# Sharing a weighted sum of gathered rows between VectorE and TensorE: more slots for TensorE in eight of 26 row tiles, another cut of the large tiles, and a new order at the end

## The chip, the cores and the metric

The kernel runs on one core of a Trainium2 chip. The metric is the device time of one execution in microseconds (us), the median of several runs. A core has engines that run side by side, each with its own in-order queue of instructions: TensorE (PE in the profile; its weight loads are a row of their own, PEld), VectorE (DVE), ScalarE (ACT), GpSimd (POOL) and SyncE (SP). Transfers run on 16 DMA engines. An engine waits for another through semaphores.

## The reference

A graph attention layer over 3327 nodes with 1024 features. The adjacency matrix is sparse: a node has between 1 and about 37 neighbours, itself included.

```python
def _L0_gnn_ref(x, adj, Wf, bf, Wg, bg, W, bW):
    f = x @ Wf + bf
    g = x @ Wg + bg
    e = jax.nn.relu(f @ g.T)
    scores = jnp.where(adj > 0, e, NEG)
    attention = jax.nn.softmax(scores, axis=1)
    x_W = x @ W + bW
    return attention @ x_W

h = jnp.maximum(_layernorm(x, axis=-1), 0.0)
x = x + _L0_gnn_ref(h, adj, ...)
```

## The kernel before

The kernel never forms the 3327 x 3327 scores. Its first part (up to about 260 us) reads x and adj, writes the normalised rows h to DRAM (`hd`), makes a list of neighbours for every row, and sorts the rows by their number of neighbours. The sorted rows are cut into 26 tiles of 128. Tile s needs `CAPS[s]` slots: slot k of a tile is the k-th neighbour of each of its 128 rows, and is fetched as one gather of 128 rows x 1024 f32 from `hd` into a buffer `G`. There are 26 such buffers.

For each tile the second part does this: `prepare` gathers the tile's own rows, transposes them on TensorE and multiplies them by A (made of Wf and Wg) to get q (24 matmuls); `dot` takes, for every slot, the dot product of the gathered row with q on VectorE; `softmax` turns the scores into weights; `combine` sums the gathered rows by their weights into y; `project` multiplies y by W (16 matmuls), and the residual x is added. A tile with more than 16 slots is done in two units, with a running softmax between them: y of the first unit is rescaled when the second unit's scores are known.

```python
CAPS = [37, 25, 23, 22, 21, 21, 20, 20, 19, 19, 18, 18, 17, 17, 17, 16, 16, 15, 15, 15, 14, 14, 13, 13, 12, 11]
ORDER = [24, *range(24), 25]
ONE_CHUNK = 16
AHEAD = 3
...
    gpool = ctx.enter_context(tc.tile_pool(name="G", bufs=26))
...
    def dot(s, k):
        e = st[s]
        g = G[s, k] = gpool.tile([P, D], FP, name="G")
        st["gathered"] = gather(g, hd[:, :], e["edges"][k])
        junk = jpool.tile([P, D], BF, name="junk")
        nc.vector.tensor_tensor_reduce(
            junk, g, e["q"][:, :D], 1.0, e["q"][:, D : D + 1], op0=ALU.mult, op1=ALU.add,
            accum_out=e["sc"][:, k : k + 1],
        )
...
    def on_tensor(s, k0, k1):
        m = min(max(0, CAPS[s] - 12), k1 - k0 - 2) if s != ORDER[0] else (k1 - k0) // 2
        ks = range(max(k0, 1), k1)
        return [k for i, k in enumerate(ks) if (i + 1) * m // len(ks) > i * m // len(ks)]

    def sum_transposed(e, g, first, last):
        ...
        for c in range(KD):          # KD = 8
            nc.tensor.matmul(
                e["yT"][:, c, :], g[:, c * P : (c + 1) * P], ident, is_transpose=True,
                start=(first and c % 4 == 0), stop=(last and c % 4 == 3), skip_group_check=True,
            )

    def combine(s, k0, k1, last):
        ...
        pe = on_tensor(s, k0, k1) if last else []
        for k in range(k0, k1):
            p = e["sc"][:, k : k + 1]
            g = G[s, k]
            if k in pe:
                nc.scalar.activation(g, g, AF.Copy, scale=p)
                sum_transposed(e, g, e["first"], False)
                e["first"] = False
            elif k == 0:
                nc.scalar.activation(y, y, AF.Copy, scale=p)
            else:
                nc.vector.scalar_tensor_tensor(y, g, p, y, op0=ALU.mult, op1=ALU.add)

    def project(s):
        e = st[s]
        yT = yTpool.tile([P, KD, P], FP, name="yT")
        sum_transposed(e, e["y"], e["first"], True)
        ...                          # copy yT_ps to yT, 16 matmuls by W_sb into ps_o, add x, scatter
```

So a slot's row is added in one of two ways. On VectorE, one `scalar_tensor_tensor` does y = g * p + y. On TensorE, ScalarE first scales the row by p, and eight 128 x 128 transposes add it, transposed, into the PSUM tile `yT`, where y itself is added at the end. `on_tensor` picks m slots of the last (or only) unit of a tile for the second way: CAPS - 12, but at most the unit's slots less two.

The units are made, and worked through, like this:

```python
    units = []
    for s in ORDER:
        cap = CAPS[s]
        half = (cap + 1) // 2
        units += [(s, 0, half), (s, half, cap)] if cap > ONE_CHUNK else [(s, 0, cap)]
    ...
    for i, (s, k0, k1) in enumerate(units):
        last = k1 == CAPS[s]
        at = ORDER.index(s)
        dots(s, range(k0, k1))
        softmax(s, k0, k1, last)
        if i + 1 < len(units):
            s2, a, b = units[i + 1]
            dots(s2, range(a, min(b, a + AHEAD)))
        if last and at:
            finish(ORDER[at - 1])
        combine(s, k0, k1, last)
        if last:
            project(s)
            if at + 2 < NT:
                prepare(ORDER[at + 2])
```

The queue of each engine is not in this order throughout: it is arranged when the program is built. The trace shows VectorE taking a sum of one unit and a dot of the next in turn.

Of the kernel before, what the change touches and what calls it, by code (L numbers as in the profile page):

```python
# [11 lines left out]
ALU = mybir.AluOpType  # L12
# [14 lines left out]
CAPS = [37, 25, 23, 22, 21, 21, 20, 20, 19, 19, 18, 18, 17, 17, 17, 16, 16, 15, 15, 15, 14, 14, 13, 13, 12, 11]  # L27

ORDER = [24, *range(24), 25]
ONE_CHUNK = 16  # L30
AHEAD = 3
LAG = 4

# [260 lines left out]
def edge_path(ctx: ExitStack, tc: tile.TileContext, x, adj, Wf, bf, Wg, bg, W, bW, out, flag):  # L294
# [11 lines left out]
    nc = tc.nc  # L306
    N, D = x.shape
# [43 lines left out]
    with ExitStack() as part1:  # L351
# [34 lines left out]
        half = c1.tile([P, 1], FP, name="half")  # L386
# [298 lines left out]
    def gather(to, table, idx, **kw):  # L685
        return nc.gpsimd.indirect_dma_start(  # L686
            out=to,
            out_offset=None,
            in_=table,
            in_offset=bass.IndirectOffsetOnAxis(ap=idx, axis=0),  # L690
            **kw,
        )
# [8 lines left out]
    st = {}  # L701
# [57 lines left out]

    G = {}  # L760

    def dot(s, k):
        e = st[s]
        g = G[s, k] = gpool.tile([P, D], FP, name="G")
        st["gathered"] = gather(g, hd[:, :], e["edges"][k])
        junk = jpool.tile([P, D], BF, name="junk")
        nc.vector.tensor_tensor_reduce(  # L767
            junk, g, e["q"][:, :D], 1.0, e["q"][:, D : D + 1], op0=ALU.mult, op1=ALU.add,
            accum_out=e["sc"][:, k : k + 1],
        )  # L770

    def dots_of_first(s, cap):

# [40 lines left out]

    def on_tensor(s, k0, k1):

        m = min(max(0, CAPS[s] - 12), k1 - k0 - 2) if s != ORDER[0] else (k1 - k0) // 2
        ks = range(max(k0, 1), k1)
        return [k for i, k in enumerate(ks) if (i + 1) * m // len(ks) > i * m // len(ks)]

    def sum_transposed(e, g, first, last):

        if first:
            e["yT"] = p_y.tile([P, KD, P], FP, name="yT_ps")
        for c in range(KD):
# [7 lines that stand above are left out]
        if not k0:  # L833
            e["y"] = G[s, 0]
        y = e["y"]
        e["first"] = True
# [8 lines that stand above are left out]
            elif k == 0:  # L845
                nc.scalar.activation(y, y, AF.Copy, scale=p)  # L846
            else:
                nc.vector.scalar_tensor_tensor(y, g, p, y, op0=ALU.mult, op1=ALU.add)  # L848

    def project(s):  # L850
        e = st[s]
# [51 lines left out]
    units = []  # L903
    for s in ORDER:
        cap = CAPS[s]
        half = (cap + 1) // 2
        units += [(s, 0, half), (s, half, cap)] if cap > ONE_CHUNK else [(s, 0, cap)]
    done = set()

    def dots(s, ks):  # L910
        for k in ks:
            if (s, k) not in done:
                done.add((s, k))
                dot(s, k)

    prepare(ORDER[0])
    prepare(ORDER[1])
# [2 lines left out]
# [15 lines that stand above are left out]
            if at + 2 == NT - 1:  # L935
                bad = failed()
# [4 lines left out]
def kernel(tc: tile.TileContext, x, adj, Wf, bf, Wg, bg, W, bW, out):  # L941

    nc = tc.nc
    with tc.tile_pool(name="flag", bufs=1) as fpool:
        flag = fpool.tile([1, 1], I32, name="flag")
        bad = edge_path(tc, x, adj, Wf, bf, Wg, bg, W, bW, out, flag)
        with tc.If(bad > 0):
            dense_path(tc, x, adj, Wf, bf, Wg, bg, W, bW, out)  # L950
# [27 lines left out]
```

## Time and profile before

| | |
|---|---|
| median of 3 runs | 1331.45 us (1329.03 to 1333.0) |
| profiled span | 1331.5 us |
| VectorE busy | 1184.0 us, 89% |
| TensorE busy, matmuls | 1105.4 us, 83% |
| ScalarE busy | 580.1 us, 44% |
| gathers of G by the lists (GpSimd) | 454, 1074 ns each |
| dots (L767) | 456, 1286 ns each |
| sums on VectorE (L848) | 296, 1289 ns each |
| row scalings for TensorE's slots (L842) | 146, 1136 ns each |
| transposes that add rows to yT (L826) | 1376 |

The profile is of one execution. A row of the groups gives the line of the kernel, the engine and operation, what is written and read, the count, then the busy time in us and the mean ns of one, then the idle time of that engine just ahead of them and what ended most of it. The row of 40 digits for an engine gives the busy tenths of 40 equal slices of the span, here 33.3 us each. TensorE's matmuls are shown in two records each for f32, and overlap: their pitch, from start to start, is shorter than one record.

### The profile page before, as it was taken

The page shows a single profiled execution, that of the slowest core. Times are in us where ns is not written, and L with a number is a line of the kernel's source. Part 1 is how long each engine was busy: PE and PEld are TensorE (multiplying, and loading weights), DVE is VectorE, ACT ScalarE, POOL GpSimd, SP SyncE. Part 2 cuts the span into 40 slices and gives each one's busy share as a digit, 9 for nine tenths or more (in the row PEclk, how much of TensorE's full clock was granted, in tenths as well). Part 3 has the DMA queues.
Part 4 walks back from the last instruction along what each step waited for, and adds up shares of the span by engine and source line. Part 5 has one row for each costly group of instructions (what it writes and reads, how often), then busy time and mean ns, then how long its engine had stood idle before and what let it go on. Part 6 is the DMA issues. An engine that isn't in the chain of part 4 may idle for free. (4 is left out here: it accounts for less than half of the span.)

```text
span 1331.5 us, 14117 instructions
## 1 busy us (share of the span) xinstructions
PE 1105.4 (83%) x4312; PEld 690.2 (52%) x4312; DVE 1184.0 (89%) x2377; ACT 580.1 (44%) x923; POOL 847.2 (64%) x677
## 2 busy tenths in 40 slices
PE   2588897289249899898999999999999997889965
PEld 2355564056136655566555656656556554545532
DVE  4779888749988999999999999999999998889990
ACT  6778787224125533555334444444433332224210
POOL 6699888356657766666666766666665655666511
PEclk9589898589669999999999999999999998899978
DMA  9999996398659988998899888988788776868811
GB/s 356 338 374 342 393 374 218 134 376 309 207 177 333 337 284 297 330 316 308 297 313 321 319 291 309 311 296 297 263 290 284 259 253 222 269 198 274 303 32 50
DMA packets 101660, 374.45 MB, mean 281 GB/s; under 512 B 14731, under 2 KB 18474, under 8 KB 98247
## 3 DMA queue, kind: packets, MB, share of 16 engines
q0 software_dynamic: 79584, 286.77, 63.4%
q1 hardware_dynamic: 11004, 71.01, 14.0%
q10 hardware_dynamic: 10986, 15.67, 3.3%
q8 instruction: 36, 0.59, 0.2%
q14 instruction: 50, 0.41, 0.1%
HBM read 344.11 MB, written 29.30 MB: 280 GB/s over the span
## 5 line engine op out<-in xcount | busy, mean ns | idle before, releaser
L686 POOL DMA_INDIRECT G<-hd,pi x454 | 487.4, 1074 | 199.2 <-issue 102.6
L767 DVE CUSTOM_DVE_ANT_0 junk<-G,q 128x1024 bf16<-128x1024 f32 x456 | 586.5, 1286 | 8.8 <-DMA G<-hd,pi 4.3
L731 PE MATMUL ps_q<-A_sb,hT 128*128 128x342 f32 x1248 | 382.1, 460 | 11.8 <-ACT hT L699 11.7
L848 DVE SCALAR_TENSOR_TENSOR G<-G,sc 128x1024 f32<-128x1024 f32 x296 | 381.4, 1289 | 10.6 <-ACT G L846 6.8
L861 PE MATMUL ps_o<-W_sb,yT 128*128 128x512 f32 x832 | 364.4, 596 | 7.9 <-ACT yT L855 7.9
L731 PEld LDWEIGHTS ps_q<-A_sb,hT 128*128 128x128 f32 x1248 | 236.2, 193 | 136.5 <-ACT hT L699 17.8
L861 PEld LDWEIGHTS ps_o<-W_sb,yT 128*128 128x128 f32 x832 | 158.0, 191 | 202.0 <-issue 187.5
L424 POOL TENSOR_TENSOR r<-r,iotaj 128x1664 f32<-128x1664 f32 (+3 forms) x52 | 191.6, 3724 | 31.9 <-ACT r L417 31.8
L826 PE MATMUL yT_ps<-ident,G 128*128 128x128 f32 x1376 | 172.5, 281 | 28.6 <-DVE G L848 15.3
L826 PEld LDWEIGHTS yT_ps<-ident,G 128*128 128x128 f32 x1376 | 155.8, 144 | 55.3 <-ACT G L842 26.4
L842 ACT ACTIVATE G<-G,sc 128x1024 f32<-128x1024 f32 x146 | 154.9, 1136 | 0.0
L475 DVE MAX8 cand<-r 128x8 f32<-128x208 f32 (+2 forms) x416 | 121.7, 360 | 29.0 <-POOL r L424 29.0
L551 PE MATMUL ps_A<-WgT,WfT 128*128 128x342 f32 x432 | 140.5, 485 | 0.2 <-ACT WfT L532 0.2
L870 ACT COPY res<-ps_o 128x512 f32<-128x512 f32 x50 | 29.2, 585 | 255.0 <-PE ps_o L861 252.8
L551 PEld LDWEIGHTS ps_A<-WgT,WfT 128*128 128x128 f32 x432 | 86.3, 205 | 60.5 <-issue 21.1
L735 ACT COPY q<-ps_q 128x342 f32<-128x342 f32 x78 | 34.3, 440 | 172.7 <-PE ps_q L731 158.7
L698 PE MATMUL ps_t<-ident,G 128*128 128x128 f32 x208 | 31.9, 303 | 80.1 <-DMA G<-hd,perm 67.5
L881 POOL DMA_INDIRECT out_dram<-res,perm x25 | 35.6, 1424 | 84.0 <-DMA res<-in_x_dram,perm 83.7
L417 ACT ACTIVATE r<-r 128x3327 f32<-128x3327 int32 (+4 forms) x28 | 77.8, 2781 | 1.5 <-ACT xt L461 0.5
L686 POOL DMA_INDIRECT res<-in_x_dram,perm x25 | 43.1, 1724 | 54.8 <-ACT res L870 49.9
L698 PEld LDWEIGHTS ps_t<-ident,G 128*128 128x128 f32 x208 | 27.3, 157 | 88.8 <-issue 74.5
L699 ACT COPY hT<-ps_t 128x512 f32<-128x512 f32 x52 | 29.2, 588 | 100.4 <-PE ps_t L698 100.4
(132 smaller groups left out, 669.4 us busy)
## 6 DMA issues: line engine op xcount, KB each, us to landing
r<-in_adj_dram SPq DMA_DIRECT2D x25, 1663.5 KB, 10.9
xt<-in_x_dram SPq DMA_DIRECT2D x25, 512.0 KB, 9.2
hd<-xt ACTq DMA_DIRECT2D x25, 512.0 KB, 7.7
G<-hd,pi POOLq DMA_INDIRECT x454, 6.2
wr<-in_L_gnn_Wg_dram SPq DMA_DIRECT2D x8, 512.0 KB, 5.8
wr<-in_L_gnn_Wf_dram SPq DMA_DIRECT2D x8, 512.0 KB, 8.1
W_sb<-in_L_gnn_W_dram SPq DMA_DIRECT2D x1, 4096.0 KB, 17.9
cd<-cand ACTq DMA_DIRECT2D x25, 64.0 KB, 7.6
```

The source lines that it names most:

```text
L417: nc.scalar.activation(r[:n, b:e], a[:n, b:e], AF.Sign, accum_out=to)
L424: nc.gpsimd.tensor_mul(r[:n, b:e], r[:n, b:e], iotaj[:n, : e - b])
L475: nc.vector.max(cand[:n, s * 8 : s * 8 + 8], r[:n, s * SW : min(N, (s + 1) * SW)])
L551: nc.tensor.matmul(ps[:, :QB], WfTs[c][:, k, :], WgT[:, k, o : o + QB], start=(k == 0), stop=(k == KD - 1))
L686: return nc.gpsimd.indirect_dma_start(out=to, out_offset=None, in_=table, in_offset=bass.IndirectOffsetOnAxis(ap=idx, axis=0), **kw,)
L698: nc.tensor.transpose(ps[:, k, :], of[:, (g + k) * P : (g + k + 1) * P], ident)
L731: nc.tensor.matmul(ps[:, :QB], hT[:, k, :], A_sb[:, k, o : o + QB], start=False, stop=(k == KD - 1), skip_group_check=True,)
L767: nc.vector.tensor_tensor_reduce(junk, g, e["q"][:, :D], 1.0, e["q"][:, D : D + 1], op0=ALU.mult, op1=ALU.add, accum_out=e["sc"][:, k : k ...
L826: nc.tensor.matmul(e["yT"][:, c, :], g[:, c * P : (c + 1) * P], ident, is_transpose=True, start=(first and c % 4 == 0), stop=(last and c % ...
L842: nc.scalar.activation(g, g, AF.Copy, scale=p)
L848: nc.vector.scalar_tensor_tensor(y, g, p, y, op0=ALU.mult, op1=ALU.add)
L861: nc.tensor.matmul(ps, yT[:, k, :], W_sb[:, k, o * CB : (o + 1) * CB], start=False, stop=(k == KD - 1), skip_group_check=True,)
```

## The change

It moves sums from VectorE to ScalarE and TensorE, and changes where a large tile is cut, so that its last unit has enough slots for TensorE's share. `FIRST` and `LARGEST` set the cut: the first unit has 10 slots, or more where the second would have over 22 (22 slots, y, and three slots of the next unit fill the 26 buffers). In the last two tiles of the order (23 and 25) the share is CAPS - 7 in place of CAPS - 12. For the last tile, the dots that are issued once the tile before has its sums are queued behind the last of those sums on VectorE.

```diff
+FIRST = 10
+LARGEST = 22
...
-    def dot(s, k):
+    def dot(s, k, behind=None):
...
-        nc.vector.tensor_tensor_reduce(
-            junk, g, e["q"][:, :D], 1.0, e["q"][:, D : D + 1], op0=ALU.mult, op1=ALU.add,
-            accum_out=e["sc"][:, k : k + 1],
-        )
+        with tc.issue_after(behind.ins) if behind else ExitStack():
+            nc.vector.tensor_tensor_reduce(
+                junk, g, e["q"][:, :D], 1.0, e["q"][:, D : D + 1], op0=ALU.mult, op1=ALU.add,
+                accum_out=e["sc"][:, k : k + 1],
+            )
...
-        m = min(max(0, CAPS[s] - 12), k1 - k0 - 2) if s != ORDER[0] else (k1 - k0) // 2
+        m = min(max(0, CAPS[s] - (7 if s in ORDER[-2:] else 12)), k1 - k0 - 2) if s != ORDER[0] else (k1 - k0) // 2
...
-                nc.vector.scalar_tensor_tensor(y, g, p, y, op0=ALU.mult, op1=ALU.add)
+                e["summed"] = nc.vector.scalar_tensor_tensor(y, g, p, y, op0=ALU.mult, op1=ALU.add)
...
-        half = (cap + 1) // 2
-        units += [(s, 0, half), (s, half, cap)] if cap > ONE_CHUNK else [(s, 0, cap)]
+        first = max(FIRST, cap - LARGEST)
+        units += [(s, 0, first), (s, first, cap)] if cap > ONE_CHUNK else [(s, 0, cap)]
...
-                dot(s, k)
+                dot(s, k, st[ORDER[-2]].get("summed") if s == ORDER[-1] else None)
```

## The prediction

> **What bounds the kernel now.** I read the page's busy tenths first, to find the stretches, and then the busy times by stretch, the groups, the waits, and the last 75 us instruction by instruction. The tenths:
>
> ```profile
> PE   2588897289249899898999999999999997889965
> DVE  4779888749988999999999999999999998889990
> PEclk9589898589669999999999999999999998899978
> ```
>
> Up to slice 8 (some 265 us) the change touches nothing. From slice 13 to 33 both VectorE and TensorE show 8 and 9; in 34 to 36 both dip; at the end VectorE falls to 0 while TensorE works on. Busy times of these stretches (columns: stretch, length, then PE, PEld, DVE, ACT, POOL, the granted clock, DMA share, GB/s):
>
> ```profile
> 385.00:440.00 55.00, 49.33 (x234) 33.85 (x234) 47.75 (x74) 27.83 (x39) 33.66 (x29) 0.93 0.78 260
> 440.00:660.00 220.00, 206.94 (x879) 134.03 (x878) 218.81 (x344) 99.14 (x157) 147.03 (x137) 0.98 0.90 313
> 660.00:960.00 300.00, 287.33 (x1207) 179.75 (x1206) 298.11 (x465) 139.68 (x225) 199.93 (x181) 0.99 0.89 305
> 960.00:1080.00 120.00, 115.58 (x425) 68.83 (x425) 113.27 (x157) 39.74 (x68) 75.07 (x69) 1.00 0.82 275
> 1080.00:1200.00 120.00, 100.42 (x363) 62.34 (x362) 99.30 (x145) 35.56 (x65) 67.70 (x56) 0.91 0.71 227
> 1258.00:1332.00 74.00, 47.59 (x120) 22.16 (x120) 39.99 (x49) 11.19 (x20) 9.77 (x8) 0.83 0.23 65
> ```
>
> From 440 to 960 us VectorE is idle for 3 us of 520: it is the bound. But TensorE is idle for only 26 us of 520, so it is nearly a second bound. The groups that the change moves between:
>
> ```profile
> L848 DVE SCALAR_TENSOR_TENSOR G<-G,sc 128x1024 f32<-128x1024 f32 x296 | 381.4, 1289 | 10.6 <-ACT G L846 6.8
> L826 PE MATMUL yT_ps<-ident,G 128*128 128x128 f32 x1376 | 172.5, 281 | 28.6 <-DVE G L848 15.3
> L842 ACT ACTIVATE G<-G,sc 128x1024 f32<-128x1024 f32 x146 | 154.9, 1136 | 0.0
> ```
>
> 296 sums on VectorE, 146 slots on TensorE; 1376 = 8 x (146 + 26), the 26 being the y of each tile. In the last 75 us, TensorE's own row of the timeline:
>
> ```profile
> 1257.95 14.00 PE L861 MATMUL ps_o<-W_sb,yT 128*128 128x512 f32 x32 [0.68 <-ACT yT L855]
> 1271.79 1.04 PE L826 MATMUL yT_ps<-ident,G 128*128 128x128 f32 x8
> 1283.70 1.97 PE L826 MATMUL yT_ps<-ident,G 128*128 128x128 f32 x8 [10.87 <-DVE G L848]
> 1286.34 15.92 PE L861 MATMUL ps_o<-W_sb,yT 128*128 128x512 f32 x32 [0.68 <-ACT yT L855]
> 1302.10 1.04 PE L826 MATMUL yT_ps<-ident,G 128*128 128x128 f32 x8
> 1304.07 14.00 PE L861 MATMUL ps_o<-W_sb,yT 128*128 128x512 f32 x32 [0.94 <-ACT yT L855]
> ```
>
> These are the projections of tiles 22, 23 and 25. TensorE stands for 10.87 us because VectorE alternates tile 23's sums with tile 25's dots, so that y of tile 23 is late. Tile 25's y is done at 1298, but its projection waits for that of tile 23.
>
> **What the Trainium skill says.** (1) "Perfetto Trace Analysis", Identifying the Most-Contended Engine: a share of matmul busy time is a bad measure of headroom. So I checked TensorE by its pitch. (2) "FP8 and Floating Point Precision", TensorE Precision Notes: true FP32 takes four passes. With the 2.4 GHz of "Trainium Kernel Development and Optimization" my estimate for a 342-column matmul is 4 x 342 / 2.4 = 570 ns. The trace has 24 of them (48 records) in 14.07 us, 586 ns each; TensorE really runs at its rate there, and its 95% is no illusion. (3) "VectorE: DVE Perf Modes", The perf-mode tier table: a two-tensor f32 operation has no faster mode. The trace agrees: 1289 ns for 1024 elements, whether dot or sum, so a sum moved away saves a whole one. (4) "TensorE: Matmul & The Clock Gate", Why this matters for your kernels: idle gaps of over about 3 us cost clock. The trace agrees: after the gap of 10.87 us the same 32 records took 15.92 us in place of 14.00.
>
> **The change, part by part.** From the rule for m, slots on TensorE go as follows. Tile 0: 16 to 20 (its last unit grows from 18 to 22 slots); tile 1: 10 to 13; tile 2: 9 to 11; tile 3: 9 to 10; tiles 4 and 5: 8 to 9 each; tile 23: 1 to 6; tile 25: 0 to 4 (11 - 7; so four, not five). Sum: 12 in the large tiles, 9 at the end, 21 in all. Tiles 10 to 14 are cut 10 + 8 or 10 + 7 in place of 9 + 9 or 9 + 8, with m unchanged. The counts should be 275 sums, 167 scalings, 1376 + 168 = 1544 transposes.
>
> A sum costs VectorE 1.20 us: in the timeline sums and dots follow each other at 1.20 us from start to start, the records overlapping a little. A slot costs TensorE 1.06 us (80 transposes of tile 2 in one run of 10.62 us) and ScalarE about 1.05 us (16 scalings of tile 0 in 16.75 us).
>
> *Large tiles.* VectorE saves 12 x 1.20 = 14.4 us, and TensorE gets 12 x 1.06 = 12.7 us more. If VectorE alone were the bound, 14.4 us would come off. I don't think so. Take tiles 1 to 5, whose cycles lie between 437 and 645 us. TensorE is busy for about 195 of these 208 us. Of its 13 idle us, 8.3 are waits for the first scaled row of a tile (that is, for VectorE's softmax), which can close; the rest is the half-microsecond wait for ScalarE's copies of hT and yT, which recurs in every tile. Eight of the twelve slots fall here, 8.5 us. New TensorE time: 195 + 8.5 + 5 = 208. TensorE becomes the bound at just the old time, and VectorE's 9.6 us turn into idle time or into a lead that later tiles, where TensorE is as full, can't use. A higher clock where gaps close (0.98 now) may give 2 to 3 us.
>
> *Tile 0.* VectorE saves 4.8 us, and its second softmax comes some 4 to 5 us earlier than 385. TensorE was idle ahead of it (342 to 385) and has room. But the 22 slots, y and three slots ahead now hold all 26 buffers, so the gathers of tile 1 and of tile 2's own rows start only when a first buffer comes free. From free to landed is about 7 us (a GpSimd issue of 1 us and 6.2 us to landing), and VectorE has only two sums and three dots to do meanwhile: I put an idle time of 6 to 9 us there, against 7 us now in the same place (its waits of 2.73, 1.88, 1.83 and 0.55 us). So of 4.8 us I keep 2 to 3.
>
> All large tiles: 0 to 10 us, I take **5**.
>
> *End.* Tile 23's scores are ready at about 1260 as now, for the first three dots of tile 25 are not held back and fill the gaps of the softmax as they did. Then six sums in a row, 7.2 us, end near 1269 in place of 1283; ScalarE scales six slots beside them. TensorE from 1258: projection of tile 22, 14.0; six slots and y, 7.4; copy of yT, 1; projection of 23, 14.0 (no cold start); 25's slots and y, 5.3; copy, 1; projection of 25, 14.0. That is 56.7 us, to 1314.7, where it was 1318.1. VectorE's way, in turn: eight dots from 1269, 10.6 us; softmax 2; y and six sums 8.4; 1290. That is earlier than TensorE can take it. So TensorE sets the end: **4 us** saved, up to 8 if the slots of 25 hide in its waits.
>
> Sum: 5 + 4, and 2 for clock and for the stretch from 1080 to 1200, where both engines lose 20 us to waits for each other that any shift may loosen or tighten: 11 us off, **1320**.
>
> **The rivals.** *(A) VectorE is the only bound.* All of 14.4 us comes off in the large tiles, and 6 to 8 at the end: 1310. For it: VectorE is idle 3 of 520 us, and its lead may be carried by the buffers until TensorE catches up after 1080. Against: TensorE's 95% at its full rate. *(B) TensorE takes over.* Nothing is gained in the large tiles and 4 us at the end: 1327; or 1333 to 1338 if the 12.7 us don't fit in the gaps, or if waiting for full buffers in tile 0 costs more than 9 us. For it: between 960 and 1080 TensorE is at 96% and VectorE only at 94%, so there it leads already. *(C) The order is what counts.* Queues are arranged anew for the whole program, and the waits of 1080 to 1200 move by up to 10 us either way. Nothing in the profile says which way.
>
> **Range and chances.** (A) and (B) put the time at 1310 to 1335, (C) adds some 5 us to each side; with 1320 between them I take 1306 to 1334. For faster by over 2% it must be below 1305, for slower by over 2% above 1358: 0.06 and 0.02; within 2%: 0.92.
>
> **What would show it.** Right: 275 sums; VectorE below 98% between 440 and 960 with TensorE at 97% or more; no idle time of 10.87 us ahead of tile 23's y on TensorE, its projection 14.0 us long, and TensorE without a gap over 3 us in the last 60 us. Tile 0: a new wait of VectorE for gathers of 6 us or more just after its second softmax. Wrong: VectorE still at 99% there with the tiles' times shorter by 1.2 us a slot (then A), or a time above the old one with TensorE waiting for transfers (then the buffers were the price).

## The result and the profile after

The changed kernel takes **1340.2 us** (median of six runs, 1337.63 to 1345.4), against 1331.65 us for the kernel before beside it (1329.03 to 1333.0). The ratio is **1.0073, 95% interval 1.0049 to 1.0096**: a small loss, where a gain of 11 us was predicted; 1320 was wrong in its sign. The profiled spans are 1331.5 and 1335.9 us. They show 4.4 us of the 8.5 us between the medians, since the profiled execution of the kernel before is a long one (1333.19 us) and that of the changed kernel the shortest of its six (1337.63 us).

The page of the changed kernel, its busy tenths:

```profile
PE   2588897189239999999999999999999998789996
DVE  3779899749979999999999999999999999888980
```

TensorE now has a 9 in every slice from 13 to 33, and again in 37 to 39, where the end was full of holes. The groups of the same page (line, engine, operation, count, then busy us and mean ns, then idle us ahead and its main releaser):

```profile
L852 DVE SCALAR_TENSOR_TENSOR G<-G,sc 128x1024 f32<-128x1024 f32 x275 | 353.5, 1286 | 21.0 <-ACT G L850 10.7
L830 PE MATMUL yT_ps<-ident,G 128*128 128x128 f32 x1544 | 192.4, 280 | 74.5 <-ACT G L846 68.1
L846 ACT ACTIVATE G<-G,sc 128x1024 f32<-128x1024 f32 x167 | 178.1, 1137 | 0.0
```

The counts are the predicted ones: 275 sums, 167 scalings, 1544 transposes. The durations of one are unchanged. TensorE's idle time ahead of the transposes seems to have grown from 28.6 to 74.5 us, but 46.7 us of it are one wait ahead of tile 0's slots, from 343 to 389 us. The kernel before had 42.6 us at the same place, put down there to the gather of tile 2's own rows, which TensorE took first. Without this wait 27.8 us are left. What has grown is the part that waits for the scaling of a row on ScalarE, which itself needs the weights from VectorE's softmax: 12.0 us before, 21.4 now.

VectorE's busy time on the page fell from 1184.0 to 1169.4 us, by 14.6; 21 sums at the pitch of 1.20 us would be 25.2. Most of the rest is in the order of its work: a dot starts 1.33 us after another dot, but a sum and a dot in turn start 1.20 us apart, and there are 182 dots right behind a dot where there were 102. At 0.13 us each that is some 10 us.

Busy times by stretch, changed kernel (stretch, length, PE, PEld, DVE, ACT, POOL, clock, DMA share, GB/s; the last stretch runs past the new end):

```profile
440.00:660.00 220.00, 205.41 (x916) 136.84 (x917) 212.11 (x330) 107.20 (x163) 146.75 (x135) 0.98 0.87 312
660.00:960.00 300.00, 285.15 (x1172) 178.88 (x1171) 292.71 (x450) 132.39 (x216) 200.80 (x179) 0.99 0.89 299
1080.00:1200.00 120.00, 103.77 (x368) 61.86 (x366) 107.45 (x155) 35.79 (x63) 65.54 (x57) 0.96 0.73 239
1258.00:1340.00 82.00, 61.20 (x229) 34.14 (x227) 39.77 (x55) 21.84 (x32) 14.44 (x12) 0.94 0.30 88
```

From 440 to 960 us VectorE is idle for 15.2 us of 520 (3 before), and TensorE for 29.4 (26 before). Neither engine is full. That is the sign to hold on to: a bound did not move from one engine to the other; **both wait more**.

**Where the time went.** I mark each tile at the reciprocal of its last softmax on VectorE (one such record per tile), and compare the marks, in us. Minus is earlier than before.

| mark of tile | before | after | difference |
|---|---|---|---|
| 0 | 389.2 | 386.8 | -2.4 |
| 4 | 575.5 | 572.6 | -2.9 |
| 10 | 808.4 | 809.1 | +0.7 |
| 15 | 972.6 | 985.8 | **+13.2** |
| 20 | 1161.7 | 1174.1 | +12.4 |
| 22 | 1227.9 | 1237.5 | +9.6 |
| end of span | 1331.5 | 1335.9 | +4.4 |

Tiles 11 to 15 cost 176.7 us in place of 164.2, though their shares are as they were. Up to tile 10 the saving of 12 sums is already gone, and VectorE is even behind: of its dots 211 are still to come after that mark, where it was 207 before. These four are made up for by tile 15, so some 5 us of the 12.5 are work that had been put off. Only the end gives something back: from the mark of tile 22 to the end 98.4 us, before 103.6.

**What is different in tile 13.** VectorE's row around tile 13's second softmax, before (from the row maximum to the scaled weights):

```profile
909.35 0.15 DVE L796 TENSOR_REDUCE nm<-sc 128x1 f32<-128x8 f32 x1
...
911.74 1.28 DVE L767 CUSTOM_DVE_ANT_0 junk<-G,q 128x1024 bf16<-128x1024 f32 x1 [0.83 <-ACT q L735]
...
913.08 1.28 DVE L767 CUSTOM_DVE_ANT_0 junk<-G,q 128x1024 bf16<-128x1024 f32 x1
...
914.40 1.28 DVE L767 CUSTOM_DVE_ANT_0 junk<-G,q 128x1024 bf16<-128x1024 f32 x1
...
915.68 0.23 DVE L810 TENSOR_SCALAR sc<-sc,rs 128x8 f32<-128x8 f32 x1
```

The same place in the changed kernel:

```profile
918.50 0.15 DVE L799 TENSOR_REDUCE nm<-sc 128x1 f32<-128x7 f32 x1
...
920.06 1.27 DVE L852 SCALAR_TENSOR_TENSOR G<-G,sc 128x1024 f32<-128x1024 f32 x1
...
921.39 1.27 DVE L852 SCALAR_TENSOR_TENSOR G<-G,sc 128x1024 f32<-128x1024 f32 x1
922.59 0.15 DVE L810 RECIPROCAL rs<-l 128x1 f32<-128x1 f32 x1
...
922.85 0.23 DVE L813 TENSOR_SCALAR sc<-sc,rs 128x7 f32<-128x7 f32 x1
924.14 1.28 DVE L852 SCALAR_TENSOR_TENSOR G<-G,sc 128x1024 f32<-128x1024 f32 x1 [1.07 <-ACT G L815]
925.35 1.28 DVE L770 CUSTOM_DVE_ANT_0 junk<-G,q 128x1024 bf16<-128x1024 f32 x1
```

Before, VectorE puts **dots of the next tile** between the steps of the softmax, and so does useful work while ScalarE makes the exponentials. In the changed kernel no dot stands there: it fills with what sums it still has, then waits 1.07 us for the rescaled y with nothing to do, and the dots come after. The reason that the times point to is on ScalarE: the copy that completes q of the next tile. Before, and then in the changed kernel:

```profile
911.26 0.45 ACT L735 COPY q<-ps_q 128x342 f32<-128x342 f32 x1
```

```profile
924.02 0.42 ACT L737 COPY q<-ps_q 128x342 f32<-128x342 f32 x1
```

A dot needs q, and q now arrives after the softmax rather than within it. I measure this for every tile as the end of q's third copy less the start of the tile's last softmax on VectorE. At the softmax of tiles 2 to 9, in order, it was -6.6, -25.2, -33.5, -24.0, -22.7, -21.3, -19.0, -2.8 us before, and is 3.4, 1.5, 3.3, 1.3, 1.0, 0.2, 3.8, 1.2 us after; at those of tiles 11 to 14, -1.3, 1.7, 3.7, 2.3 before and 6.2, 8.3, 7.2, 7.2 after. **In tiles 3 to 8 q lost a lead of some 20 us or more, because TensorE now does it behind the projection.** The added slots alone are too few for this: tiles 1 to 5 have eight more, 8.5 us. The order of TensorE's queue changed with them. TensorE around tile 3 before: q of tile 5 (in two records for each of 24 matmuls), then tile 3's slots and y, then tile 3's projection.

```profile
520.88 14.07 PE L731 MATMUL ps_q<-A_sb,hT 128*128 128x342 f32 x48 [0.29 <-ACT hT L699]
538.82 10.62 PE L826 MATMUL yT_ps<-ident,G 128*128 128x128 f32 x80 [3.87 <-ACT G L842]
550.36 14.00 PE L861 MATMUL ps_o<-W_sb,yT 128*128 128x512 f32 x32 [0.92 <-ACT yT L855]
```

In the changed kernel tile 3's slots and projection come first, and nearly all of tile 5's q after them:

```profile
533.73 11.33 PE L830 MATMUL yT_ps<-ident,G 128*128 128x128 f32 x88 [3.32 <-ACT G L846]
...
546.05 13.89 PE L865 MATMUL ps_o<-W_sb,yT 128*128 128x512 f32 x32
559.78 12.81 PE L733 MATMUL ps_q<-A_sb,hT 128*128 128x342 f32 x44
```

So it is for all of tiles s = 2 to 7: before, q of tile s+2 is complete 2.4 to 14.9 us ahead of the projection of tile s, and in the changed kernel 21 to 28 us after its start. The queues are arranged when the program is built; three runs of one kernel on three chips (e2, e2b, e2c below) have their records in the same order on both engines. So the lateness of q is in large part an order that the build chose. What made it choose so is not shown.

VectorE's queue shows the same. I count the dots that start between the first record of a tile's last softmax and the scaling of its scores: before, three to five in each of tiles 1 to 14; in the changed kernel none in tiles 1 to 4, one to three in tiles 5 to 9, and none in tiles 10 to 14, at whose marks the time is lost. How late q is does not decide it alone: before, tiles 12 to 14 had three dots there with q up to 3.7 us late, and tile 3 of the changed kernel has none with 1.5.

The circle closes on TensorE. Its waits from 806 to 980 us, which hold tiles 11 to 15, before (engine, what waited for what, us in total, times, longest):

```profile
PE ps_q L731 <- ACT hT L699: 5.0, 4, 1.9
PE yT_ps L826 <- ACT G L842: 1.5, 2, 1.0
```

and in the changed kernel:

```profile
PE yT_ps L830 <- ACT G L846: 12.1, 11, 2.7
```

TensorE stands 12.1 us for the first weighted rows, which the later softmax of VectorE sets; VectorE's softmax has no dots, and TensorE's q is late for them. The theory taken into the experiments (**Q**): the larger share makes q late, and that costs more than the sums save. Its rivals: the new cut of the small tiles 10 to 14 (**C** below; the prediction's C was wider, the order of all queues), and TensorE simply full (**B**, called T at q1).

### The profile page after: what moved, and what is told of

It reads as the page before. It is cut to its first block, busy times and chain, and to the rows that moved or that the text cites. A ratio compares the mean times of both kernels' runs of the same rounds, so it can differ in the third digit from the quotient of the medians.

```text
span 1335.9 us, 14463 instructions
## 1 busy us (share of the span) xinstructions
PE 1118.7 (84%) x4480; PEld 708.6 (53%) x4480; DVE 1169.4 (88%) x2356; ACT 601.5 (45%) x944; POOL 844.8 (63%) x677
## 4 chain that ended last, share of the span: by engine, by line
DVE 29%; issue 26%; PE 17%; DMA 11%; POOL 11%; ACT 5%; POOLq 0%; ACTq 0%; DVEq 0%; SPq 0%
DVE G L852 14%; DMA G<-hd,pi 6%; PE ps_o L865 6%; DVE junk L770 6%; POOL r L426 5%; PE ps_q L733 5%; POOL G L688 4%; PE yT_ps L830 4%; DVE cand L477 4%; ACT G L846 1%; PE ps_A L553 1%; DMA G<-hd,perm 1%; DVE sc L770 1%; ACT r L419 1%; DMA bgT<-in_L_gnn_bg_dram 1%
## 5 line engine op out<-in xcount | busy, mean ns | idle before, releaser
L733 PE MATMUL ps_q<-A_sb,hT 128*128 128x342 f32 x1248 | 377.6, 457 | 11.9 <-ACT hT L701 11.9
L852 DVE SCALAR_TENSOR_TENSOR G<-G,sc 128x1024 f32<-128x1024 f32 x275 | 353.5, 1286 | 21.0 <-ACT G L850 10.7
L830 PE MATMUL yT_ps<-ident,G 128*128 128x128 f32 x1544 | 192.4, 280 | 74.5 <-ACT G L846 68.1
L830 PEld LDWEIGHTS yT_ps<-ident,G 128*128 128x128 f32 x1544 | 173.8, 144 | 100.7 <-ACT G L846 82.9
L846 ACT ACTIVATE G<-G,sc 128x1024 f32<-128x1024 f32 x167 | 178.1, 1137 | 0.0
L803 ACT ACTIVATE sc<-sc,nm 128x10 f32<-128x10 f32 (+10 forms) x41 | 12.5, 305 | 125.5 <-DVE nm L801 73.3
L688 POOL DMA_INDIRECT pi<-pd,perm x26 | 33.6, 1292 | 53.0 <-DMA G<-hd,pi 31.5
## 6 DMA issues: line engine op xcount, KB each, us to landing
r<-in_adj_dram SPq DMA_DIRECT2D x25, 1663.5 KB, 10.5
```

What stands on the lines that cost most here:

```text
L688: return nc.gpsimd.indirect_dma_start(out=to, out_offset=None, in_=table, in_offset=bass.IndirectOffsetOnAxis(ap=idx, axis=0), **kw,)
L733: nc.tensor.matmul(ps[:, :QB], hT[:, k, :], A_sb[:, k, o : o + QB], start=False, stop=(k == KD - 1), skip_group_check=True,)
L830: nc.tensor.matmul(e["yT"][:, c, :], g[:, c * P : (c + 1) * P], ident, is_transpose=True, start=(first and c % 4 == 0), stop=(last and c % ...
L852: e["summed"] = nc.vector.scalar_tensor_tensor(y, g, p, y, op0=ALU.mult, op1=ALU.add)
```

## The experiments

On the chips of e1, e2, e3, e5 and of their repeats with b, the kernel before itself took 1352 to 1396 us, so their ratios are to the runs beside them, and their inner times are used only from tile 7 on; the repeats with c, e4 and the q runs had quiet chips.

**The parts of the change, one at a time.** The small cut alone (tiles 10 to 14 cut 10 + 8 or 10 + 7), in the kernel before:

```diff
-        half = (cap + 1) // 2
+        half = (cap + 1) // 2 if cap > 18 else 10
```

> The kernel before, with the tiles of 17 and 18 slots (10 to 14) cut at 10, as the change does; shares on TensorE as before (no sum moves). Theory Q (TensorE's added slots make the next tile's q late, VectorE then has no dots to put between the steps of the second softmax, and each bare softmax costs 2 to 3 us): no slots are added, so most of the loss stays away; 1333 to 1337, and only where the second unit has 7 slots (tiles 12 to 14) is the softmax bare. Rival C (the cut itself costs: with 9 sums against 7 or 8 dots the first unit's sums outlast the dots and push the second softmax back): the 12 us that the changed kernel loses in tiles 11 to 15 come back whole, 1341 to 1345.

> The same kernel as e1_small_cut (tiles 10 to 14 cut at 10, shares as before), taken again for the same reason. Theory Q: 2 to 6 us slower than before, part of it at the end, where the softmaxes of tiles 23 and 25 stand bare in VectorE's order. Rival C: 10 us slower or more by tile 15.

Measured: ratios 1.0087 (1.0044 to 1.013) and 1.0191 (1.0106 to 1.0276), slower by the equivalent of 12 and 25 us, which is nearer to what C expected. But its own five tiles, 11 to 15, take 167.0 and 166.5 us, only some 2.5 more than the 164.2 before. From the mark of tile 20 to that of 25 it takes 129.6 and 122.8 us, where the profile of the kernel before has 120.5. So the small cut does not make the 12.5 us of tiles 11 to 15; and an edit in tiles 10 to 14 seems to move tiles 21 to 25, which it does not touch, by 2 to 9 us.

The large cut with the share that follows it, but nothing at the end and the small tiles as before:

```diff
-        half = (cap + 1) // 2
+        half = (cap + 1) // 2 if cap < 21 else max(10, cap - 22)
```

> The kernel before, with the new cut and so the larger share only in the tiles of 21 and more slots (0 to 5): 12 sums go from VectorE to TensorE, the small tiles are cut as before and the end is as before. Theory Q: VectorE's second softmax is bare from tile 1 on and stays so in the later tiles, for TensorE's lag isn't made up; 1336 to 1341. Rival C: the small tiles are cut as before, so nothing is lost there; 1327 to 1332. What the prediction said (TensorE becomes the bound at just the old time): 1331 less 2 to 3.

> The same kernel as e2_large_only (new cut and larger share in tiles 0 to 5 alone), taken again because on the chip of that run even the kernel before spread from 1352 to 1396 us. Theory Q (added slots delay the next tile's q, the second softmax stands bare in tiles 1 to 5 and 11 to 14): slower by 4 to 9 us than before. What the prediction said: faster by 2 to 5 us. Rival C (the small tiles' cut alone is at fault): faster or the same.

> New cut and larger share in tiles 0 to 5 alone; the small tiles and the end as before. Theory Q: tiles 11 to 15, cut as before, still take some 176 to 181 us in place of 164, since TensorE's lag from the large tiles stays and the softmax there is bare; the whole is 10 to 18 us slower than before. Rival C: tiles 11 to 15 take 164 to 167 us; no loss.

Measured: 1.0182 (1.0078 to 1.0286), 1.0199 (1.0116 to 1.0283), and on a quiet chip 1345.78 us against 1330.46, 1.0108 (1.0067 to 1.0148). Tiles 11 to 15 take 179.2, 181.1 (in an execution of 1408.97 us, the longest of that run) and 177.7 us. The first two lost more than expected, the third 15.3 us, as expected. This part carries the whole loss. In e2c q is as late as in the changed kernel (3.4, 1.5, 3.3, 1.3 us after the softmax of tiles 2 to 5 begins), and TensorE's wait for the first scaled rows in tiles 11 to 15 is there too:

```profile
PE yT_ps L826 <- ACT G L842: 11.3, 6, 3.3
```

The end alone: the changed kernel with the old cut everywhere, which also takes back the share of the large tiles.

```diff
-        first = max(FIRST, cap - LARGEST)
+        first = (cap + 1) // 2
```

> The changed end alone (five and four more slots in tiles 23 and 25, the last dots behind the sums), all tiles cut as before. All theories: the interval from the last softmax but one to the end shortens as in the changed kernel, by 5 to 6 us: 1325 to 1327. If it's slower, the end too is not what it seemed.

> The same kernel as e3_end_only (the changed end alone), taken again for the same reason. All theories: 5 to 6 us faster than before, since VectorE's order up to tile 22 is the same as before.

Measured: 0.9998 (0.9951 to 1.0046), which shows nothing of the expected gain, and 0.9944 (0.9905 to 0.9982), which does. In e3b the stretch from the mark of tile 22 to the end is 97.1 us, where it was 103.6: 6.5 us saved, which is the end's part, and tiles 11 to 15 (165.5) are as before.

The large cut **without** the larger share: m held at the value that it has with the old cut (tile 0 is left with its rule).

```diff
-        half = (cap + 1) // 2
+        half = (cap + 1) // 2 if cap < 21 else max(10, cap - 22)
...
-        m = min(max(0, CAPS[s] - 12), k1 - k0 - 2) if s != ORDER[0] else (k1 - k0) // 2
+        m = min(max(0, CAPS[s] - 12), CAPS[s] // 2 - 2 if 20 < CAPS[s] else k1 - k0 - 2) if s != ORDER[0] else (k1 - k0) // 2
```

> The kernel before, with the new cut in the tiles of 21 and more slots, but their old number of slots on TensorE (16, 10, 9, 9, 8, 8): the cut without the share. Theory Q: TensorE gets nothing more, q is as early as before, dots stand between the steps of the softmax; 1328 to 1333. A rival for the large tiles (the long second units fill the buffers, and gathers come late): slower by 3 us or more, with VectorE waiting for gathers in tile 1.

> The same kernel as e5_large_cut_old_share (new cut in tiles 0 to 5, old number of slots on TensorE), taken again for the same reason. Theory Q: within 3 us of before, dots stand between the steps of the second softmax from tile 3 on. Full-buffer rival: slower by 3 us or more, with VectorE waiting for gathers in tile 1.

> The same cut in tiles 0 to 5 with the old number of slots on TensorE. Theory Q: tiles 11 to 15 take 164 to 167 us, as before, and the whole is within 6 us of before; the difference to e2c, 8 us or more, is what the larger share costs. Rival (the long second units and their buffers cost): as slow as e2c.

Measured: 1.0116 (1.0039 to 1.0193), 1.0181 (1.0093 to 1.027), and on a quiet chip 1340.36 us, 1.0072 (1.0042 to 1.0103). The time was a miss: I had not expected the cut by itself to cost. Nor is e5c 8 us faster than e2c, as Q expected; it is 5.4 us faster. Inside, though, it separates two things. Tiles 11 to 15 take 164.3 us, as before, and q is early again (-6.8, -20.3, -24.8, -23.8 us at the softmax of tiles 3 to 6). What e5c loses, it loses ahead of that: at the mark of tile 6 it is 10.5 us behind the kernel before, at that of tile 15 10.7. VectorE's waits from 389 to 670 us, before:

```profile
DVE junk L767 <- DMA G<-hd,pi: 4.3, 4, 1.9
DVE G L848 <- ACT G L812: 2.7, 1, 2.7
DVE l L804 <- ACT al L803: 0.2, 1, 0.2
```

and in e5c:

```profile
DVE junk L767 <- DMA G<-hd,pi: 4.7, 3, 2.7
DVE G L848 <- ACT G L812: 4.2, 2, 3.1
DVE mask L740 <- DMA pi<-pd,perm: 2.6, 1, 2.6
DVE l L804 <- ACT al L803: 1.4, 2, 0.7
DVE junk L767 <- DMA G<-hd,more: 0.6, 1, 0.6
```

That is 13.5 us in place of 7.2: some six of the ten, spread over lists, gathers and bare softmax steps. Most of the rest is work that moved: tile 0's longer second unit leaves six sums to VectorE in place of two, and these come after tile 0's mark, where 277 sums are left in place of 273. Four sums are 4.8 us, and the mark itself came only 1.7 us earlier for them. I have no run that isolates these. The rival of full buffers thus has the size that it expected, but its sign only in part: the waits for gathers and lists are 7.9 us in place of 4.3.

Two runs of one chip, e2c and e5c, thus differ in the share alone, and their marks give its price and its yield (us, behind the kernel before; tile 24 comes first, ahead of anything that was changed, and shows how far two executions differ anyway; both profiled executions are the longest of their run):

| | tile 24 | tile 0 | tile 6 | tile 10 | tile 15 | tile 20 |
|---|---|---|---|---|---|---|
| e5c, cut alone | +0.3 | -1.7 | +10.5 | +10.6 | +10.7 | +12.2 |
| e2c, cut and share | -1.6 | -3.3 | -0.7 | -0.3 | +13.2 | +16.3 |
| the share's part | -1.8 | -1.7 | -11.1 | -10.9 | **+2.5** | +4.1 |

The share gains 9.5 us between the marks of tiles 0 and 6, where VectorE has twelve sums less to do (14.4 us; four are tile 0's), and loses 13.4 in tiles 11 to 15. Part of this loss is older than it looks: at the mark of tile 10 the kernels with the larger share have four dots more to do than the others. By the medians, the cut costs 9.9 us (1330.46 to 1340.36) and the share another 5.4 (to 1345.78; the intervals of the two ratios overlap). **Nearly two thirds of the loss of this part is thus the cut's, and the share, which was to save up to 14.4 us, saves nothing.**

The changed kernel with the small tiles cut as before:

```diff
-        first = max(FIRST, cap - LARGEST)
+        first = max(FIRST, cap - LARGEST) if cap > 18 else (cap + 1) // 2
```

> The changed kernel with the tiles of 17 and 18 slots cut as before; large tiles and end as changed. Theory Q: tiles 11 to 15 still take 174 us or more, and the whole is within 5 us of the changed kernel (1335 to 1342 where before takes 1332). Rival C: the 12 us come back, 1326 to 1330.

Measured: 1343.74 us, 1.0103 (1.0066 to 1.0139), just above what Q expected; tiles 11 to 15 177.8 us. Rival C falls for the 12.5 us: they are there with the old cut of just these tiles.

**q early.** If Q holds, the same share must be harmless once q no longer waits for it. In the changed kernel I issue `prepare` of the tile after next ahead of the projection, which nothing but the output waits for. Nothing is left out.

```diff
         if last:
-            project(s)
             if at + 2 < NT:
                 prepare(ORDER[at + 2])
+            project(s)
```

> The changed kernel, with prepare(tile s+2) ahead of project(tile s) in the code, so that TensorE does the q of the tile after next before the projection, which nothing on VectorE waits for. The work is the same. Theory Q (late q leaves the second softmax bare): in VectorE's queue dots stand between the steps of the softmax again from tile 1 on; the cycles of tiles 7 to 15, 294 us in the changed kernel, fall to 286 or less, and the whole is 8 to 18 us faster than the changed kernel. Rival C (the cut at 10 of the small tiles costs by itself): tiles 10 to 14 stay at 36 to 38 us each. Rival T (TensorE's plain amount of work is the bound, as the prediction said): no gain over the changed kernel, since TensorE has the same work.

Measured: **1321.48 us against 1332.15, ratio 0.9917 (0.9893 to 0.9942)**: faster than both kernels, with the sums, slots and cut of the changed one; this refutes B, as the amount of TensorE's work is the same. q comes 2.5 to 13.3 us ahead of the start of the softmax in every tile from 1 to 14. VectorE's row in tile 13:

```profile
911.44 0.15 DVE L799 TENSOR_REDUCE nm<-sc 128x1 f32<-128x7 f32 x1
911.51 1.27 DVE L770 CUSTOM_DVE_ANT_0 junk<-G,q 128x1024 bf16<-128x1024 f32 x1
...
914.00 1.27 DVE L770 CUSTOM_DVE_ANT_0 junk<-G,q 128x1024 bf16<-128x1024 f32 x1
...
918.03 0.22 DVE L813 TENSOR_SCALAR sc<-sc,rs 128x7 f32<-128x7 f32 x1
918.17 1.28 DVE L770 CUSTOM_DVE_ANT_0 junk<-G,q 128x1024 bf16<-128x1024 f32 x1
```

The dots are back between the steps, three to five of them in every tile from 1 to 14, and no wait stands in the row. Tiles 11 to 15 take 164.1 us, with three dots fewer to make up for than in the changed kernel, and TensorE's wait for the first scaled rows there is down:

```profile
PE yT_ps L830 <- ACT G L846: 3.4, 8, 0.8
```

The swap does something of its own, however, so it must be measured without the share: the end-only kernel with the same swap.

```diff
-        first = max(FIRST, cap - LARGEST)
+        first = (cap + 1) // 2
...
         if last:
-            project(s)
             if at + 2 < NT:
                 prepare(ORDER[at + 2])
+            project(s)
```

> The changed end alone (old cut, old shares in the large tiles), with q ahead of the projection as in q1. Theory Q: before tile 10 nothing is won, as dots stood in the softmax already; in tiles 15 to 20, where softmaxes are bare in the kernel before, some 5 us may be won or lost; 5 to 10 us faster than before, and within 8 us of q1. If the larger share pays once q is early, q1 is faster than this one by 5 us or more.

Measured: 1330.03 us, 0.9982 (0.9965 to 0.9998), a smaller gain than expected; the end alone with the projection first had 0.9998 and 0.9944 (e3, e3b, on less quiet chips). So the swap by itself brings nothing that these runs can tell. On one chip, the new cut and the larger share are thus worth 8.6 us of medians once q is first (1330.03 to 1321.48), where with the projection first they lose. Two things keep this from being a clean size. q3 takes 172.6 us in tiles 11 to 15, although in tiles 11 to 14 q is 12 to 15 us early and four or five dots stand in each softmax: it waits 6.5 us there for the factor `al` from ScalarE, another place for the same softmax to stand. It is in these tiles that the profiled q1 passes q3: at the mark of tile 10 it is 3.4 us behind, at that of tile 15 5.1 ahead. And both q1 and q3 are fast in tiles 16 to 20 (173.6 and 175.3 us, before 189.1), where VectorE's waits for the exponentials between 1080 and 1200 us have gone; this is the line before,

```profile
DVE rs L807 <- ACT sc L800: 18.2, 4, 6.2
```

and this is q1's:

```profile
DVE rs L810 <- ACT sc L803: 1.3, 4, 0.3
```

So that gain belongs to the order of the two calls, not to the share. And q1 still has room: in tiles 1 to 10 it takes 427.3 us, where the kernel before takes 419.2, with 14.3 us of VectorE's waits for gathers in the whole second part (8.5 in the changed kernel).

The swap with the old cut of the small tiles:

```diff
-        first = max(FIRST, cap - LARGEST)
+        first = max(FIRST, cap - LARGEST) if cap > 18 else (cap + 1) // 2
...
         if last:
-            project(s)
             if at + 2 < NT:
                 prepare(ORDER[at + 2])
+            project(s)
```

> q1 (the changed kernel with q ahead of the projection) with the tiles of 17 and 18 slots cut as before. The small cut alone cost 2.5 us in tiles 11 to 15; if it still does with early q, this is 1 to 4 us faster than q1, a ratio of 0.988 to 0.991 to before; if early q covers it, the same as q1 (0.992).

Measured: 1319.38 us against 1330.46, 0.9912 (0.9882 to 0.9943), with q1 within the error. The small cut matters neither way.

**Less work for TensorE.** The direct test of B: leave out half of the 16 matmuls by W in both kernels. Their outputs lack half of y times W, and TensorE has 7 us less to do per tile.

```diff
-            for k in range(KD):
+            for k in range(KD - 4, KD):
```

> The changed kernel with half of the projection left out (four of eight matmuls into each bank; the output is not y times W then): TensorE has some 7 us less in every tile. To be read against r2, the kernel before with the same left out. Theory Q: with TensorE relieved, q is early, and the moved sums pay in full: 14 us in the large tiles, 5 at the end; r1 is 12 to 20 us faster than r2. Rival C: the small tiles' cut still costs 10 us; r1 is within 8 us of r2.

> The kernel before with the same half of the projection left out. Theory Q: VectorE was the bound up to tile 14 and stays so; little is won up to there (0 to 5 us), more in tiles 15 to 20, where VectorE waited, and at the end, where two half projections are 14 us less: 1290 to 1310 on a chip where before takes 1331.

Measured: r1 (changed kernel) 1348.1 us, 1.0131 (1.0078 to 1.0185); r2 (kernel before) 1357.57 us, 1.0194 (1.0144 to 1.0245). **Both are slower than the kernel before with its whole work.** My expectation for r2 failed outright. Between the two, the changed kernel is the faster one, by 9.5 us, which goes the way of Q but stays short of the number; and the dots stand again between the softmax steps of r1. But more than the load was changed: the granted clock fell. Two stretches of r1, 440 to 660 and 960 to 1080 us:

```profile
440.00:660.00 220.00, 178.95 (x843) 125.36 (x842) 203.79 (x318) 105.56 (x159) 145.40 (x130) 0.90 0.84 295
960.00:1080.00 120.00, 88.13 (x359) 57.84 (x358) 106.48 (x160) 43.12 (x69) 68.03 (x60) 0.87 0.75 250
```

0.90 and 0.87, where it was 0.98 and 1.00. The Trainium skill, "TensorE: Matmul & The Clock Gate", section HAM oscillation, tells of a kernel whose short bursts of matmuls between waits let the clock drop again each time; a TensorE with holes in it and a lower clock agree with that here (0.872 and 0.868 in the mean of r1 and r2), though no run shows which holes did it. And VectorE's waits for the exponentials rose from 19.1 us before to 39.2 (r1) and 45.3 (r2) between 307 and 1300 us. Tiles 11 to 15 take 180.7 us in r1 and 178.0 in r2, although q is 20 to 36 us early there and three to five dots stand in each softmax: at this lower clock, an early q alone does not make these tiles fast. These two runs are inconclusive for the size of anything.

## Why the prediction was wrong, point by point

- **Counts and prices of one instruction: right; what a sum saves: too high.** 275, 167 and 1544; the records of a sum, a scaling and a transposed row are as long as before. But "a sum moved away saves a whole one" held only while sums and dots still alternated. In e2c twelve sums fewer took 5.8 us off VectorE's busy time (1184.0 to 1178.2), not 14.4. Likewise six sums in a row took 7.9 us at the end, not 7.2.
- **Tile 0: the wait was right, what was left of the saving is not shown.** A wait for gathers of 6 to 9 us just after the second softmax was predicted, against 7 us of waits there before, with 2 to 3 us left of the saving. The one wait is 6.55 us; from the mark of tile 0 to that of tile 1 VectorE is idle for 10.6 us in place of 7.4. The mark of tile 0, 2.4 us earlier, lies ahead of that wait:

```profile
397.50 1.29 DVE L770 CUSTOM_DVE_ANT_0 junk<-G,q 128x1024 bf16<-128x1024 f32 x1 [6.55 <-DMA G<-hd,pi]
```

- **The end: right.** Predicted 4 us, up to 8, with a chain of 56.7 us on TensorE. TensorE's row in the changed kernel:

```profile
1268.77 14.00 PE L865 MATMUL ps_o<-W_sb,yT 128*128 128x512 f32 x32 [1.62 <-ACT yT L859]
1282.61 6.28 PE L830 MATMUL yT_ps<-ident,G 128*128 128x128 f32 x56
1290.20 14.00 PE L865 MATMUL ps_o<-W_sb,yT 128*128 128x512 f32 x32 [1.31 <-ACT yT L859]
1304.04 4.53 PE L830 MATMUL yT_ps<-ident,G 128*128 128x128 f32 x40
1309.24 14.00 PE L865 MATMUL ps_o<-W_sb,yT 128*128 128x512 f32 x32 [0.67 <-ACT yT L859]
```

  From 1268.77 to 1323.24 us that is 54.5 us, before 60.1. The gap of 10.87 us is gone, the projection of tile 23 takes 14.00 in place of 15.92, and no gap is over 1.62. The saving is 5.2 us from tile 22's mark here and 6.5 in e3b.
- **Large tiles: this step failed.** It read: "TensorE becomes the bound at just the old time, and VectorE's 9.6 us turn into idle time or into a lead that later tiles, where TensorE is as full, can't use." It put TensorE's 12.7 us into its gaps: of 13 idle us between 437 and 645 us, the 8.3 that wait for a tile's first scaled row "can close". They did not close. In the changed kernel they are 8.9 us, and TensorE is idle for 13.1 us of that stretch, as before. The step asked what TensorE's own end would do, and not who **lives on TensorE's lead**. Before, q of the next tile came 19 to 34 us early in six of the tiles, and dots that had their q filled VectorE's softmax. With the new cut and share TensorE's queue has the projection ahead of q and this lead is gone; then VectorE idled 15.2 us in place of 3, TensorE waited for VectorE's weights, and TensorE's busy share went *down*, from 95.1% to 94.3% of the 520 us. The predicted sign "VectorE below 98%" came (97.1%), its other half, "TensorE at 97% or more", did not: the two halves together would have been a full TensorE, which was not there. Taken -5, measured +0.7 at tile 10 and +13.2 at tile 15.
- **"Tiles 10 to 14 ... with m unchanged": the loss fell where the prediction had none.** Not for their cut (e4): q is late there too, and the dots that were missing in the softmax are done after it. Of the 12.5 us, VectorE's idle time makes 5.7 (7.7 of 176.7 us, before 2.0 of 164.2); the rest is more busy time: four dots more and one sum less between the marks, and 51 dots right behind a dot in place of 17.
- **The large cut itself: not priced.** The prediction charged it to tile 0 alone. e5c puts it at 10 us, lost in tiles 1 to 6: more than the changed kernel loses in all.
- **2 us for clock and 1080 to 1200: not found.** That stretch gained 8 us of VectorE's busy time, and the clock there went from 0.91 to 0.96, but tiles 16 to 20 take 188.3 us in place of 189.1.
- **The rivals.** A fell. B came nearest in size (1333 to 1338 with a price for buffers) but not in mechanism: no full TensorE. C, that the new order of the queues is what counts, comes closest to what the traces show, but was set aside with "nothing in the profile says which way". The profile did show what was at stake, by how long ahead of the softmax q was copied; that the new order would give this up, it could not show.

What stays open: why the cut alone costs 10 us, beyond the waits and the four sums counted above; how many of the 13.4 us in tiles 11 to 15 are the bare softmax steps and how many the debt of four dots; and why q3 loses 8 us in tiles 11 to 15. The swap shows that the kernel with the same cut and share is faster than before once q is first. As it arranges all queues anew and changes other waits too, how much of the loss is late q's alone is not shown; no run has the larger share with VectorE's and TensorE's old order.

## What to carry to other kernels

An engine with no idle time may still be giving others a lead, and the lead is a resource: before adding work to it, take each thing that it makes for others and measure how long ahead of its first use it is ready. If the lead is what fills somebody's waits, price its loss, not only the added busy time. And in an in-order queue, put the work that another engine waits for (here q) ahead of the work that only the output waits for (here the projection): with that order the kernel with the same cut and share took 0.9917 of the time of before. Where the build arranges the queues, read from the trace which order it chose; a small edit can turn it round.

## What the runs showed of the hardware that was not expected

Taking half of the projection from TensorE made the kernel slower, 1.3% and 1.9%, with a mean granted clock of 0.87, where the kernel before had 0.92 to 0.94 on that chip. On VectorE, a dot starts 1.33 us after another dot and a sum 1.32 us after another sum, but a sum and a dot in turn start 1.20 us apart. A dot is followed by a record of 0.08 us that reads its accumulator; a sum starts together with that record, a second dot only after it. Sums have no such record, so it does not explain the sums in a row. The same dots and sums cost more busy time in rows of a kind than in turn.
